# A graph attention layer on one core: where output parts are moved, and how the last two batches of edges are summed

## The chip, the cores and the metric

The kernel runs on one core of a Trainium2 chip. The metric is device time in microseconds (us) for one execution: the median of several runs. A core has a matrix engine (PE), a vector engine (DVE), an activation engine (ACT), a general engine (Pool) and a queue engine (SP); each works through its own queue in order and waits for others by semaphores. PE reads SBUF and writes PSUM; DVE and ACT read and write both. A matmul on float32 appears as two records in the trace.

## The reference, cut to what matters

A layer of graph attention: 12,500 nodes of 128 features, 412,500 edges sorted by target, 4 heads of 32.

```python
h = (relu(layernorm(x)) @ W_node.T).reshape(num_nodes, H, HD)
e = (edge_attr_64 @ W_edge.T).reshape(num_edges, H, HD)
att = leaky(sum(concat([h[src], h[tgt], e]) * a))         # one value an edge and head
m = max(segment_max(att, tgt), 0.0)
ex = exp(att - m[tgt])
denom = segment_sum(ex, tgt) + (num_edges - deg) * exp(-m)
out = x + segment_sum((ex / denom[tgt]) * h[src], tgt)
```

## The kernel before, in words

A first stage normalizes the nodes and writes a table to HBM with one row of 144 floats a node: per head the 32 projected features, two ones and the source's share of the attention value (AW = 35 floats a head, 140 in all), then the target's shares.

The edges are cut into 461 chunks of 896, and the chunks into 58 batches of 8 (CB); the last batch, number 57, has 5 chunks, the fifth of 3 tiles instead of 7 (a tile is 128 edges). NBT is 58. For each batch these steps run:

- `load` and `gather` (L469 to L502): SP fetches edge features and targets; Pool issues one indirect DMA a tile (L500), 56 a batch, that brings the sources' table rows into `hs`. There are two `hs` buffers. From the third batch on a small Pool copy, `gate` (L498), stands in front of a batch's gathers; it reads `sums`, which ACT writes when the batch that last used this buffer has been summed.
- `begin` (L509 to L534): masks (`mem`, `hot`) on DVE and attention values `z` on PE (L518, L521).
- `weigh` (L536 to L565): once all rows have landed, DVE transposes the sources' shares (L541), and DVE and ACT compute leaky values, running maxima and exponentials. It ends with two transposes on DVE (L563, L564).
- `scatter` (L567 to L590): DVE multiplies each chunk's rows by their exponentials (L578, one instruction a chunk); PE then sums the edges of a chunk into its 32 target rows, one matmul a tile (L586), with the mask `hot` as weights. Three chunks (G = 3) go together: a matmul with 96 weight columns and 420 moving columns, of whose nine 32x140 blocks only the three on the diagonal are wanted. In the last two batches the step is one chunk: 32 weight columns, 140 moving columns. The PSUM tile `pa` has two buffers which take turns.
- `collect` (L594 to L609): ACT copies the wanted blocks, four of 32x35 a chunk, from PSUM to the tile `r` (L609). In the last batch's last chunk every other copy is DVE's (L607).
- `merge` (L611 to L656): DVE and ACT join the chunks' sums of one or two batches and add them to `acc`. Batches 0 to 55 are merged in pairs, 56 and 57 each by itself.
- `finish` (L696 to L733): when all edges of some blocks of 128 nodes are in, they are divided by the denominator (`wgt`), brought from the layout (head, node in window) by rows to the layout (node) by rows, added to x and stored. The change of layout is 16 matmuls against parts of the identity (L721), four heads times four partition groups, each in a column group of PE of its own by `tile_position`; DVE adds from PSUM (L726). `parts()` cuts the 98 blocks into thirteen parts of 7, one of 5 and one of 2. The parts of 7 are done behind batches 5, 9, 13 and so on to 53, the part of 5 behind batch 56, that of 2 behind 57. The stores are issued one batch later.

The order is the program's own (`manual_schedule`). In iteration b stand: load and gather of batch b + 1, weigh of b, stores, scatter of b, begin of b + 1, merge of b, finish. So every engine's queue has batch b's scatter, merge and part in front of batch b + 1's weigh. The code behind the loop (`window`) handles chunks whose targets spread too far; with this data it runs no time.

## Time and profile before

| what | us |
|---|---|
| median of 3 runs | 4163.02 (4162.63 to 4165.32) |
| the profiled execution's own time | 4160.05 |
| its span, first to last instruction | 4157.8 |
| Pool busy | 3073.5, of it L500 3047.1 in 3223 gathers |
| DVE busy | 1814.1 |
| PE busy | 1538.9, of it L586 906.3 |
| ACT busy | 645.9, of it L609 385.3 in 1842 copies |

The span begins and ends with the first and last instruction; a little of the time lies around it. The mean granted PE clock over the span is 0.678 of full speed. Rows of the timeline give the start in us, the duration, engine, line, operation, output and input, the number of instructions merged into the row, and in brackets the idle time in front and what ended it.

### The profile page before, as it was taken

What the parts mean: (1) busy time and instruction counts of PE and PEld (TensorE: products, weight loads), DVE (VectorE), ACT (ScalarE), POOL (GpSimd) and SP (SyncE); (2) the same over time, 40 slices, a digit from 0 to 9 for tenths busy, and PEclk for the clock granted to TensorE, in tenths of its full rate; (3) what the DMA queues carried; (4) which work ended last, traced back from release to release, by engine and by line L of the source; (5) the groups of instructions that cost most, each with busy time, mean ns of one, the idle gap of its engine ahead of it and who ended that gap; (6) DMA issues with size and microseconds to landing.
All of it is one profiled execution on the core that took longest, in us unless ns stands there. A gap on an engine that the chain in (4) does not pass through costs nothing.

```text
span 4157.8 us, 24120 instructions
## 1 busy us (share of the span) xinstructions
PE 1538.9 (37%) x4721; PEld 637.2 (15%) x4721; DVE 1814.1 (44%) x3336; ACT 645.9 (16%) x2553; POOL 3073.5 (74%) x3337
## 2 busy tenths in 40 slices
PE   5324252424242524243434333333333242424243
PEld 4101120111110201111111111111111111111112
DVE  8244444434442534353435343534353434434445
ACT  5111111111111111111111111111111111111111
POOL 3777777777777777777777777777777777777774
PEclk8667676767676766666666666676767676767676
DMA  6433433333333333334333333333333333333331
GB/s 183 135 92 96 127 113 94 113 98 107 101 109 99 103 110 94 118 89 118 94 114 98 114 93 118 89 119 94 114 98 114 93 118 90 117 96 109 101 108 51
DMA packets 243629, 440.90 MB, mean 106 GB/s; under 512 B 93947, under 2 KB 144119, under 8 KB 243479
## 3 DMA queue, kind: packets, MB, share of 16 engines
q0 software_dynamic: 103136, 237.83, 21.8%
q1 hardware_dynamic: 127030, 194.11, 14.0%
q10 hardware_dynamic: 13312, 7.36, 0.6%
q8 instruction: 45, 0.74, 0.1%
q14 instruction: 106, 0.86, 0.1%
HBM read 423.75 MB, written 15.29 MB: 106 GB/s over the span
## 4 chain that ended last, share of the span: by engine, by line
POOL 71%; issue 25%; DVE 2%; DMA 1%; PE 1%; ACT 0%; POOLq 0%; DVEq 0%; ACTq 0%
POOL hs L500 71%; DMA hs<-table,src 1%; PE pa L586 1%; DVE stats L265 0%; POOL gate L498 0%; DVE hT L311 0%; DMA table<-rows 0%; DVE hn L297 0%; PE ph L316 0%; PE pt L306 0%; DMA pens<-pen 0%; DVE dif L274 0%; DVE acc L656 0%; DMA xg<-in_x 0%; PE up L721 0%
## 5 line engine op out<-in xcount | busy, mean ns | idle before, releaser
L500 POOL DMA_INDIRECT hs<-table,src x3223 | 3047.1, 945 | 978.2 <-issue 969.3
L586 PE MATMUL pa<-hs,hot 128*96 128x420 f32 (+2 forms) x2526 | 906.3, 523 | 2434.8 <-issue 2345.9
L586 PEld LDWEIGHTS pa<-hs,hot 128*96 128x96 f32 (+2 forms) x2526 | 421.2, 171 | 2931.9 <-issue 2792.2
L541 DVE STREAM_TRANSPOSE zst<-hs 128x224 f32<-128x224 f32 x58 | 33.6, 579 | 1651.6 <-DMA hs<-table,src 1651.6
L609 ACT COPY r<-pa 32x35 f32<-32x35 f32 x1842 | 385.3, 209 | 820.4 <-PE pa L586 800.6
L578 DVE TENSOR_TENSOR hs<-hs,exr 128x924 f32<-128x924 f32 x461 | 476.8, 1101 | 0.0
L550 ACT ACTIVATE a<-z 32x224 f32<-32x224 f32 x232 | 80.5, 347 | 2046.2 <-DVE z L549 2046.2
L518 PE MATMUL z<-eft,wa 128*32 128x384 f32 (+1 forms) x928 | 361.5, 543 | 21.7 <-DMA twb<-table 21.7
L533 DVE TENSOR_TENSOR hot<-exr,key 128x448 f32<-128x448 f32 x231 | 138.7, 622 | 351.8 <-PE pa L586 347.3
L521 PE MATMUL z<-mem,twb 128*32 128x512 f32 x464 | 185.2, 542 | 3.3 <-DMA twb<-table 3.3
L559 ACT ACTIVATE both<-a 32x224 f32<-32x224 f32 x232 | 89.9, 388 | 370.1 <-DVE a L556 365.8
L518 PEld LDWEIGHTS z<-eft,wa 128*32 128x32 f32 x928 | 97.7, 110 | 269.3 <-issue 269.3
L513 DVE TENSOR_TENSOR mem<-mem,exr 128x896 f32<-128x896 int32 x116 | 120.3, 1074 | 18.9 <-DMA mem<-in_dstc 18.9
L549 DVE TENSOR_TENSOR z<-z,zst 32x224 f32<-32x224 f32 x232 | 89.7, 387 | 81.6 <-ACT a L550 76.2
L656 DVE TENSOR_TENSOR acc<-acc,a 128x70 f32 x461 | 109.0, 236 | 33.1 <-DVE acc L656 18.2
L553 DVE TENSOR_TENSOR_SCAN up<-pen,z 32x896 f32<-32x896 f32 x58 | 117.0, 2016 | 2.0
L555 DVE TENSOR_TENSOR_SCAN m<-pen,up 32x896 f32<-32x896 f32 x58 | 116.4, 2007 | 2.0
L561 DVE SCALAR_TENSOR_TENSOR both<-pen,m 32x224 f32<-32x224 f32 x232 | 88.0, 379 | 2.4
L721 PE MATMUL up<-a,ident 128*32 128x224 f32 (+2 forms) x480 | 43.8, 540 | 96.1 <-DVE a L714 96.1
L551 DVE TENSOR_TENSOR z<-z,a 32x896 f32<-32x896 f32 x58 | 63.0, 1087 | 24.0 <-ACT a L550 24.0
L521 PEld LDWEIGHTS z<-mem,twb 128*32 128x32 f32 x464 | 51.2, 110 | 128.0 <-issue 117.4
L556 DVE TENSOR_TENSOR a<-z,m 32x896 f32<-32x896 f32 x58 | 62.5, 1078 | 2.0
(140 smaller groups left out, 732.1 us busy)
## 6 DMA issues: line engine op xcount, KB each, us to landing
eft<-in_ef SPq DMA_DIRECT2D x58, 1792.0 KB
mem<-in_dstc SPq DMA_DIRECT2D x116, 448.0 KB
hs<-table,src POOLq DMA_INDIRECT x3223, 2.5
twb<-table SPq DMA_DIRECT2D x464, 0.5 KB
pen<-pens SPq DMA_DIRECT2D x58, 112.1 KB
xg<-in_x SPq DMA_DIRECT2D x14, 448.0 KB
table<-rows ACTq DMA_DIRECT2D x9, 648.0 KB
out<-xg SPq DMA_DIRECT2D x13, 448.0 KB
```

The lines of the kernel that those rows point to most:

```text
L500: nc.gpsimd.indirect_dma_start(out=s.hs[:, i, :], out_offset=None, in_=table[:, :], in_offset=bass.IndirectOffsetOnAxis(ap=s.src[:, i:i + ...
L513: nc.vector.tensor_tensor(s.mem[:, k, :], s.mem[:, k, :].bitcast(I32), nid_ps[:, pair:pair + 1].to_broadcast([P, CE]), op=OP.is_equal)
L518: nc.tensor.matmul(s.z[:, part], wa3[:, j, :], s.eft[:, j, part], start=(j == 0), stop=False)
L521: nc.tensor.matmul(s.z[:, part], twb[:, s.b % 2, k, :], s.mem[:, k, part], start=False, stop=(k == 1))
L533: nc.vector.tensor_tensor(hot[:, :, q0:q0 + 2, :].rearrange("p t q r -> p q t r"), rows_ps[:, None, None, :].to_broadcast([P, 2, T, W]), k ...
L553: nc.vector.tensor_tensor_scan(up, s.pen[:, :CE], s.z, 0.0, op0=OP.add, op1=OP.max)
L555: nc.vector.tensor_tensor_scan(m[:, ::-1], s.pen[:, CE:0:-1], up[:, ::-1], 0.0, op0=OP.add, op1=OP.max)
L559: nc.scalar.activation(both[g * R:(g + 1) * R, 0, :, :], grouped(att, g), AF.Exp)
L578: nc.vector.tensor_tensor(rows, rows, ex_ps[:, :n, q * H:(q + 1) * H, None].to_broadcast([P, n, H, HB]), op=OP.mult)
L586: nc.tensor.matmul(pa[:v * W, :v * H * AW], hot[:, i, q0:q0 + v, :].rearrange("p q r -> p (q r)"), by_chunk[:, q0:q0 + v, i, :], start=(i ...
L609: nc.scalar.copy(to, pa[q * W:(q + 1) * W, k:k + AW])
L656: nc.vector.tensor_tensor(cols, cols, put[:, i0 + i, :, :], op=OP.add)
```

## The change

Three edits. `finish` gets a flag `by_act`, set for parts behind batches below 56: the 16 matmuls become 16 ACT copies from `w4` to the same places in PSUM. Batch 56 goes in steps of G = 3 as the batches in front of it do. Batch 57 goes in steps of two chunks; chunk q is summed in column group q % 4 of PE into PSUM rows of its own, slot q // 4, the matmuls of the two chunks alternating, and all five chunks use one PSUM tile. `collect` is handed the blocks to copy in place of the tile.

```diff
@@ scatter
-        step = G if s.b + 2 < NBT else 1
+        single = s.b + 1 == NBT
+        step = 2 if single else G
+        if single:
+            one = ps.tile([P, G * H * AW], F32, name="pa", bufs=2)
+            by_slot = one[:, :2 * H * AW].rearrange("p (j k) -> p j k", j=2)
...
+            if single:
+
+                for i in range(T):
+                    for q in range(q0, q0 + w):
+                        if i < held[q]:
+                            g = q % 4
+                            nc.tensor.matmul(by_slot[g * W:(g + 1) * W, q // 4, :], hot[:, i, q, :], by_chunk[:, q, i, :],
+                                             start=(i == 0), stop=(i == held[q] - 1), tile_position=(0, g * W))
+                collect(s, q0, w, [by_slot[q % 4 * W:(q % 4 + 1) * W, q // 4, :] for q in range(q0, q0 + w)])
+                continue
...
-            order = [0, *range(n, T if w > 1 else n), *range(1, n)]
+            order = [0, *range(n, T), *range(1, n)]
...
-            collect(s, q0, w, pa)
+            collect(s, q0, w, [pa[q * W:(q + 1) * W, q * H * AW:(q + 1) * H * AW] for q in range(w)])
@@ collect
-    def collect(s, q0, w, pa):
+    def collect(s, q0, w, blocks):
...
-                k = (q * H + h) * AW
+                what = blocks[q][:, h * AW:(h + 1) * AW]
                 if s.b == NBT - 1 and q0 + w == s.chunks and h % 2:
-                    nc.vector.tensor_copy(to, pa[q * W:(q + 1) * W, k:k + AW])
+                    nc.vector.tensor_copy(to, what)
                 else:
-                    nc.scalar.copy(to, pa[q * W:(q + 1) * W, k:k + AW])
+                    nc.scalar.copy(to, what)
@@ finish
-    def finish(pool, psum, tag, em, b0, n):
+    def finish(pool, psum, tag, em, b0, n, by_act=False):
...
         for h in range(H):
             for s in range(4):
+                if by_act:
+                    nc.scalar.copy(po[s * W:(s + 1) * W, h // 2, h % 2, :n, :], w4[h * W:(h + 1) * W, :n, s, :])
+                    continue
                 nc.tensor.matmul(po[s * W:(s + 1) * W, h // 2, h % 2, :n, :],
...
@@ the loop over batches
-                    stores.append(finish(work, ps, "up", em_ps, b0, n))
+                    stores.append(finish(work, ps, "up", em_ps, b0, n, b + 2 < NBT))
```

More of the change, by code (lines that the diff above doesn't have):

```diff
@@ L579, in scatter @@
                     rows, rows, ex_ps[:, :n, q * H:(q + 1) * H, None].to_broadcast([P, n, H, HB]), op=OP.mult)
+            if single:
[7 more added lines that the diff above has]
+                continue
             pa = ps.tile([P, G * H * AW], F32, name="pa", bufs=2)
             n = held[q0 + w - 1]
-            order = [0, *range(n, T if w > 1 else n), *range(1, n)]
+            order = [0, *range(n, T), *range(1, n)]
             for i in order:
                 v = w if i < n else w - 1
-                nc.tensor.matmul(pa[:v * W, :v * H * AW], hot[:, i, q0:q0 + v, :].rearrange("p q r -> p (q r)"), by_chunk[:, q0:q0 + v, i, :],
-                                 start=(i == order[0]), stop=(i == order[-1]))
-            collect(s, q0, w, pa)
+                nc.tensor.matmul(pa[:v * W, :v * H * AW], hot[:, i, q0:q0 + v, :].rearrange("p q r -> p (q r)"),
+                                 by_chunk[:, q0:q0 + v, i, :], start=(i == order[0]), stop=(i == order[-1]))
+            collect(s, q0, w, [pa[q * W:(q + 1) * W, q * H * AW:(q + 1) * H * AW] for q in range(w)])
     merged = {}
-    def collect(s, q0, w, pa):
+    def collect(s, q0, w, blocks):
         first, last = merge_of(s.b)
         if s.b + 2 < NBT and q0 + w == s.chunks:
-            nc.scalar.copy(sums, pa[:W, 0:1])
+            nc.scalar.copy(sums, blocks[-1][:, 0:1])
         if s.b == first and q0 == 0:
```

## The prediction

> **What bounds the kernel now.** I read the shares by engine first, then the chain of waits, then the group of the gathers, then the last 140 us in order of time. The first three say that Pool's gathers set the pace:

> ```profile
> PE 1538.9 (37%) x4721; PEld 637.2 (15%) x4721; DVE 1814.1 (44%) x3336; ACT 645.9 (16%) x2553; POOL 3073.5 (74%) x3337
> ...
> POOL 71%; issue 25%; DVE 2%; DMA 1%; PE 1%; ACT 0%; POOLq 0%; DVEq 0%; ACTq 0%
> ...
> L500 POOL DMA_INDIRECT hs<-table,src x3223: 940/944/1923, 80.2 to 4111.1; - x190
> ...
> L541 DVE STREAM_TRANSPOSE zst<-hs 128x224 f32<-128x224 f32 x58 | 33.6, 579 | 1651.6 <-DMA hs<-table,src 1651.6
> ```

> From 80 us to 4112 us Pool issues 3223 gathers of 0.945 us with 0.30 us of its own issue time between them, 1.25 us apiece (3223 x 1.25 = 4029). The shortest takes 0.940, the median 0.944, and busy time less count times median is 3047.1 - 3042.5 = 4.6 us: contention costs Pool next to nothing, so relieving it can give next to nothing. DVE waits for the gathers at the head of nearly every batch, 1651.6 / 57 = 29 us a time. The one wait that could stop Pool is the gate copy (L498), which reads `sums`, written at the end of the scatter before. In order of time:

> ```profile
> 4036.58 0.15 ACT L596 COPY sums<-pa 32x1 f32<-32x1 f32 x1 [0.85 <-PE pa L586]
> ...
> 4073.10 0.20 POOL L498 COPY gate<-sums 32x1 f32<-32x1 f32 x1
> ```

> `sums` is there 36.5 us before the gate reads it. So up to the last gather every other engine has room, and only what follows batch 56's arrival can be read as time. There the chain leaves Pool:

> ```profile
> 4074.74 0.58 DVE L541 STREAM_TRANSPOSE zst<-hs 128x224 f32<-128x224 f32 x1 [21.00 <-DMA hs<-table,src]
> ...
> 4087.18 0.58 DVE L564 STREAM_TRANSPOSE hs<-both 128x224 f32<-128x224 f32 x1
> ...
> 4088.97 15.58 PE L586 MATMUL pa<-hs,hot 128*32 128x140 f32 x112 [43.35 <-DVE hs L578]
> ...
> 4105.49 0.17 DVE L621 TENSOR_SCALAR mc<-r 128x8 f32<-128x8 f32 x1 [3.46 <-ACT r L609]
> ...
> 4111.14 0.99 POOL L500 DMA_INDIRECT hs<-table,src  x1 [0.30 <-issue]
> ...
> 4116.33 0.57 DVE L541 STREAM_TRANSPOSE zst<-hs 128x224 f32<-128x224 f32 x1
> ...
> 4130.34 9.42 PE L586 MATMUL pa<-hs,hot 128*32 128x140 f32 x62 [14.88 <-issue]
> ...
> 4140.70 0.21 DVE L607 COPY r<-pa 32x35 f32<-32x35 f32 x1 [0.28 <-ACT r L609]
> ```

> Batch 57's last gather starts at 4111.14 and lands 2.47 us later (as the one at 4072.15 did, by the chain), at 4113.6; its weighing starts at 4116.33 with no idle time in front, because DVE is still busy with batch 56's merge and output part. So batch 56 already ends last, by 2.7 us, and what is added to it from 4088 on is paid in full, as is what is added to batch 57. What stands behind 4140.9 (merge, output part, store) keeps its instructions.

> **The change part by part. (1) Output by ACT copies.** `by_act` holds for the parts behind batches below 56: the thirteen of seven blocks. The parts behind 56 and 57 keep their matmuls. Each of the thirteen loses 16 matmuls and gains 16 copies of 32x224, each waiting for the one before by a semaphore. No row has this copy. Nearest below is a PSUM-to-SBUF ACT operation of that shape (L550, 0.347), nearest above the Exp of that shape with the same wait on ACT (L559: four in 1.62, 0.405 apiece); a SBUF-to-PSUM operation of 528 elements (L629) took 0.61 and is a far upper bound. I take 0.405: 16 x 0.405 = 6.5 us (5.6 to 9.8) against 3.3 us of PE. DVE's L726 waits 3.2 us longer (2.3 to 6.5). In ACT's queue stands next only the following batch's L550, in DVE's the following L541. What hides it: after the part at 3912 DVE idles 17.96 us before L541. If that cover were gone, the 36.5 us of the gate come next; a copy would have to take (3.3 + 18 + 36.5) / 16 = 3.6 us to stop Pool. The last such part is behind batch 53, so none reaches the tail. The SP queue is unmoved: the store is issued an iteration later, behind the pen load. Cost 0.

> **(2) Batch 56 in threes.** Removed: 56 matmuls of 140 columns and eight collects of 4 copies; added: 21 matmuls (14 of 420, 7 of 280 columns) and collects of 12, 12 and 8. Batch 55 already ran so:

> ```profile
> 4017.22 0.58 DVE L564 STREAM_TRANSPOSE hs<-both 128x224 f32<-128x224 f32 x1
> ...
> 4021.01 15.48 PE L586 MATMUL pa<-hs,hot 128*96 128x420 f32 x42 [44.74 <-issue]
> ...
> 4038.42 0.17 DVE L621 TENSOR_SCALAR mc<-r 128x16 f32<-128x16 f32 x1 [1.12 <-ACT r L609]
> ```

> PE's time is the same (15.48 against 15.58), since three times the columns take three times as long. But PE begins after three multiplies instead of one, and 8 copies instead of 4 follow its last matmul. From L564's start to L621: 21.20 in threes, 18.31 in ones; less 0.1 for the `sums` copy that batch 56 lacks, **+2.8 us**, all of it on the path. The bounds come from the same two rows, +2.5 to +3.0. The z matmuls of batch 57 end 2.0 us later, at 4115.6, still ahead of their reader, now at 4119.7.

> **(3) Batch 57 by column groups, in pairs.** Same 31 matmuls (62 records), but pairs of chunks alternate between two column groups, all in one PSUM tile. Two costs and one gain. Cost: the pair's alternation stops at its second matmul until the second multiply, 1.0 us later (4131.3 on the old clock). Cost: in the instruction order of the changed program the first matmul of pair 2, and that of the fifth chunk, wait for a count on ACT which only the last copy of the pair before brings; the tile is tracked as a whole. Before, two tiles took turns and PE never stopped. Queued behind the waiting matmul is all of the scatter. Gain: groups may overlap. The windows show what decides the sizes (us, PE, PEld, DVE, ACT, POOL, then the granted clock):

> ```profile
> 4114.17:4115.46 1.29, 1.29 (x32) 0.97 (x32) 0.00 (x0) 0.00 (x0) 0.00 (x0) 1.00 0.04 13
> 4115.50:4130.30 14.80, 0.00 (x0) 0.00 (x0) 12.57 (x19) 2.94 (x8) 0.00 (x0) 0.55 0.10 28
> 4130.34:4133.80 3.46, 3.46 (x15) 2.63 (x16) 3.45 (x4) 0.00 (x0) 0.00 (x0) 0.50 0.00 0
> 4133.80:4135.70 1.90, 1.90 (x16) 1.71 (x15) 0.00 (x0) 0.83 (x4) 0.00 (x0) 0.90 0.00 0
> 4135.70:4139.80 4.10, 4.06 (x35) 3.48 (x32) 0.00 (x0) 2.36 (x12) 0.00 (x0) 1.00 0.00 0
> ```

> A record of 140 columns takes 3.45 / 14 = 0.246 at clock 0.50 and 1.67 / 14 = 0.119 at 1.00. The output part's 32 records of 160 columns over four groups took 0.040 each where 160 / 140 x 0.119 = 0.136 would be one alone: 3.4-fold overlap on four groups. For two groups I take 1.9 (bounds 1 and 2). Overlap bought at the price of copies in series then gives, on the old clock: pair 1 from 4131.3, 26 records x 0.246 / 1.9 = 3.4, to 4134.7; 8 copies 1.8 (batch 55's eight took 1.76), to 4136.5; pair 2 at full clock 28 x 0.119 / 1.9 = 1.75, with 0.1 for the wait to 4138.4 (at half clock 3.6, to 4140.2); copies, 1.8; chunk five, 6 records, 0.7 or 1.5; its four copies, alternating between ACT and DVE, 0.95. End 4141.9 with the clock up, 4144.5 with it down, against 4140.9: +1.0 to +3.6. A stretch's mean clock dates the step in it: 0.90 over 1.90 us puts the rise at 4134.2, 3.8 us after PE started; 0.55 over 14.8 us puts the fall 1.5 us after PE stopped; 0.80 over the 7.8 us behind 4139.8 puts the next fall 4.7 us after. So a gap of 1.8 us may or may not drop it. I take pair 2 at full clock and chunk five at half, **+1.8 us**.

> [...]

> **Sum:** 0 + 2.8 + 1.8 = +4.6 us, on the profiled execution's 4157.8 span and 4160.05 time (2.97 below the median shown, 4163.02). On the median: 4167.6, or 0.11% up. Own bounds: +2.5 + 0.7 (two-fold overlap) to +3.0 + 3.6, that is 4166.2 to 4169.6.

> **Rivals.** (A) Nothing lost in batch 57: the copies of a pair hide after all, or pair 1 gets the full clock early. Then overlap wins 1.5 us (PE ends at 4137.3, last copies at 4139.4) and the sum is +1.3: 4164.3. For it: overlap is in the trace. Against it: the wait on ACT is in the program. (B) Slower: the two groups do not overlap and every gap drops the clock. Place: the last batch; 26, 28 and 6 records at 0.246 make 14.8 us of PE, with 3.8 of copies between and 0.95 behind from 4131.3: end 4150.8, +9.9, with batch 56 +12.7: 4175.7. It decides "slower" from +5.5 us in this stage on. Against it: the 3.4-fold overlap, and that continuous work raised the clock within 4.2 us each time. Without overlap but with the clock up from pair 2 on it is some 7 us in sum, 4170. (C) ACT's copies stop the gathers: 3.6 us a copy needed, 0.4 expected; each further us per copy would then cost 13 x 16 = 208 us. (D) Faster by more than 8 us: the whole contention of the gathers is 4.6 us, so nothing in the profile pays for it.

> **How the numbers follow.** Forecast 0.76; A 0.09; B 0.10 with its milder form; C 0.01; D 0.04. What a measurement here can tell from no change is about 0.2%, 8.3 us, so forecast, A and the milder half of B are "same": 0.87, with 0.09 slower and 0.04 faster. The time is the forecast's, 4167.6; the range runs from below A, by the runs' own spread of 1 us, to between B's two forms: 4163.3 to 4172.

> **What would show it.** Gathers unchanged at 0.945 and 1.25 apart; the thirteen copies groups near 6.5 us with DVE still idle some 15 us before L541; batch 56 with L564 to L621 near 21; batch 57's L541 near 4119; PE there in three bursts, with gaps of about 1.9 us that end with ACT. I am wrong if the span moves by more than 8 us, if Pool waits at a gate, or if PE's last scatter has no gaps.

## The result, and the profile after

The changed kernel took 4169.92 us in the median of 20 runs (4167.26 to 4171.43), the kernel before 4163.53 (4161.63 to 4165.32): a ratio of 1.0015, 95% interval 1.0009 to 1.0021, so 4 to 9 us longer. The forecast was 4167.6, or 4.6 us more than the 4163.02 it started from; the medians of 20 runs differ by 6.4 us.

The profiled execution took 4170.56 us, its span is 4168.8. First the page of the changed kernel: shares of the chain of waits, then groups (busy us and mean ns of one, then the idle time in front and what ended it).

```profile
POOL 72%; issue 24%; DVE 2%; PE 1%; DMA 1%; ACT 0%; SPq 0%; POOLq 0%; DVEq 0%; ACTq 0%
...
L500 POOL DMA_INDIRECT hs<-table,src x3223 | 3050.7, 947 | 978.2 <-issue 972.6
...
L541 DVE STREAM_TRANSPOSE zst<-hs 128x224 f32<-128x224 f32 x58 | 33.6, 578 | 1616.8 <-DMA hs<-table,src 1616.8
...
L736 ACT COPY up<-a 32x224 f32<-32x224 f32 x208 | 70.7, 340 | 33.4 <-DVE a L728 27.2
```

Pool still sets the pace, and DVE still waits 1616.8 / 57 = 28 us for each batch's gathers. The part behind batch 53 in order of time, first in the kernel before:

```profile
3915.38 1.16 DVE L726 TENSOR_TENSOR xg<-up,xg 128x448 f32<-128x448 f32 x2 [3.42 <-PE up L721]
...
3934.50 0.58 DVE L541 STREAM_TRANSPOSE zst<-hs 128x224 f32<-128x224 f32 x1 [17.96 <-DMA hs<-table,src]
```

then in the changed kernel:

```profile
3918.11 5.92 ACT L736 COPY up<-a 32x224 f32<-32x224 f32 x16 [2.09 <-DVE a L728]
...
3924.06 1.16 DVE L743 TENSOR_TENSOR xg<-up,xg 128x448 f32<-128x448 f32 x2 [6.04 <-ACT up L736]
...
3940.58 0.58 DVE L541 STREAM_TRANSPOSE zst<-hs 128x224 f32<-128x224 f32 x1 [15.36 <-DMA hs<-table,src]
```

Sixteen copies take 5.92 us; DVE's add waits 6.04 us instead of the 3.42 it waited for PE, and the idle time in front of the next transpose falls from 17.96 to 15.36: 2.6 us taken out of slack, nothing out of the end. The last two batches:

```profile
4093.33 0.58 DVE L564 STREAM_TRANSPOSE hs<-both 128x224 f32<-128x224 f32 x1
...
4097.11 16.27 PE L600 MATMUL pa<-hs,hot 128*96 128x420 f32 x42 [45.53 <-issue]
...
4115.22 0.27 DVE L635 TENSOR_SCALAR mc<-r 128x8 f32<-128x8 f32 x1 [3.94 <-ACT r L623]
...
4117.05 1.11 POOL L500 DMA_INDIRECT hs<-table,src  x1 [0.30 <-issue]
...
4126.15 0.57 DVE L541 STREAM_TRANSPOSE zst<-hs 128x224 f32<-128x224 f32 x1
...
4138.53 0.58 DVE L564 STREAM_TRANSPOSE hs<-both 128x224 f32<-128x224 f32 x1
...
4140.16 0.65 PE L590 MATMUL pa<-hs,hot 128*32 128x140 f32 x2 [14.87 <-issue]
4141.13 3.04 PE L590 MATMUL pa<-hs,hot 128*32 128x140 f32 x26 [0.33 <-DVE hs L582]
4144.21 1.75 ACT L623 COPY r<-pa 32x35 f32<-32x35 f32 x8 [6.17 <-PE pa L590]
4146.01 1.86 PE L590 MATMUL pa<-hs,hot 128*32 128x140 f32 x28 [1.84 <-ACT r L623]
4147.95 1.78 ACT L623 COPY r<-pa 32x35 f32<-32x35 f32 x8 [1.99 <-PE pa L590]
4149.78 0.90 PE L590 MATMUL pa<-hs,hot 128*32 128x140 f32 x6 [1.91 <-ACT r L623]
```

Batch 56 takes 21.89 us from L564 to the merge's first reader of the copies, where the ones took 18.31. Batch 57's transpose has no idle time in front, 9.1 us behind its last gather's start (5.2 before): the delay is paid in full. In batch 57 PE runs its first two records, and the third waits for the second multiply; then PE works in three bursts, and both gaps between them, 1.84 and 1.91 us, end with ACT: PE and ACT take turns. From L541 of batch 56 to the end of the span it is 87.9 us, 83.1 before: **+4.85 us** in the stretch that holds the edits to the last two batches. The rest of this pair of profiles, 6.15 us in front of that, is no step of the change: the first gather starts 2.4 us later (82.69 against 80.25) and first to last gather is 3.5 us longer (4034.4 against 4030.9). The experiments say how far these two belong to the change.

### The profile page after: what moved, and what is told of

Read it like the earlier page. It is cut to its first block, busy times and chain, and to the rows that moved or that the text cites. A ratio compares the mean times of both kernels' runs of the same rounds, so it can differ in the third digit from the quotient of the medians.

```text
span 4168.8 us, 23404 instructions
## 1 busy us (share of the span) xinstructions
PE 1496.2 (36%) x4235; PEld 608.4 (15%) x4235; DVE 1813.4 (43%) x3336; ACT 722.2 (17%) x2761; POOL 3077.2 (74%) x3337
## 4 chain that ended last, share of the span: by engine, by line
POOL 72%; issue 24%; DVE 2%; PE 1%; DMA 1%; ACT 0%; SPq 0%; POOLq 0%; DVEq 0%; ACTq 0%
POOL hs L500 71%; PE pa L600 0%; DVE stats L265 0%; DMA hs<-table,src 0%; POOL gate L498 0%; DMA table<-rows 0%; PE ph L316 0%; DVE hT L311 0%; DVE hn L297 0%; PE pa L590 0%; PE pt L306 0%; ACT r L623 0%; DMA twb<-table 0%; DMA pens<-pen 0%; DVE acc L670 0%
## 5 line engine op out<-in xcount | busy, mean ns | idle before, releaser
L500 POOL DMA_INDIRECT hs<-table,src x3223 | 3050.7, 947 | 978.2 <-issue 972.6
L600 PE MATMUL pa<-hs,hot 128*96 128x420 f32 (+1 forms) x2394 | 895.6, 537 | 2553.8 <-issue 2510.1
L600 PEld LDWEIGHTS pa<-hs,hot 128*96 128x96 f32 (+1 forms) x2394 | 406.7, 175 | 3054.4 <-issue 2918.9
L541 DVE STREAM_TRANSPOSE zst<-hs 128x224 f32<-128x224 f32 x58 | 33.6, 578 | 1616.8 <-DMA hs<-table,src 1616.8
L550 ACT ACTIVATE a<-z 32x224 f32<-32x224 f32 x232 | 80.5, 347 | 1939.5 <-DVE z L549 1939.5
L559 ACT ACTIVATE both<-a 32x224 f32<-32x224 f32 x232 | 89.9, 388 | 370.0 <-DVE a L556 365.8
L561 DVE SCALAR_TENSOR_TENSOR both<-pen,m 32x224 f32<-32x224 f32 x232 | 87.9, 379 | 2.4
L736 ACT COPY up<-a 32x224 f32<-32x224 f32 x208 | 70.7, 340 | 33.4 <-DVE a L728 27.2
L551 DVE TENSOR_TENSOR z<-z,a 32x896 f32<-32x896 f32 x58 | 63.0, 1087 | 23.9 <-ACT a L550 23.9
```

The lines of the kernel that those rows point to most:

```text
L500: nc.gpsimd.indirect_dma_start(out=s.hs[:, i, :], out_offset=None, in_=table[:, :], in_offset=bass.IndirectOffsetOnAxis(ap=s.src[:, i:i + ...
L559: nc.scalar.activation(both[g * R:(g + 1) * R, 0, :, :], grouped(att, g), AF.Exp)
L600: nc.tensor.matmul(pa[:v * W, :v * H * AW], hot[:, i, q0:q0 + v, :].rearrange("p q r -> p (q r)"), by_chunk[:, q0:q0 + v, i, :], start=(i ...
```

## The experiments

Each kernel was timed beside the kernel before on the same chip. The three groups ran on three different chips: beside `e1` to `e4` and `e9` to `e12` the kernel before took 5116 and 5112 us, beside `e5` to `e8` it took 4160. Where it took over 5100 the matrix engine is at times far slower, also while batch 56 is weighed (23.9 us from its L541 to its L564 in `e12_before_again`, 12.4 in the first profile), but not from that L564 on, 70 to 76 us before the end. So the scatters of the last two batches can be read from all of the profiles, total times only against the kernel before of the same group.

**One part at a time.** `e1_act_only` is the kernel before with the edit to `finish` alone:

```diff
-    def finish(pool, psum, tag, em, b0, n):
+    def finish(pool, psum, tag, em, b0, n, by_act=False):
...
             for s in range(4):
+                if by_act:
+                    nc.scalar.copy(po[s * W:(s + 1) * W, h // 2, h % 2, :n, :], w4[h * W:(h + 1) * W, :n, s, :])
+                    continue
                 nc.tensor.matmul(po[s * W:(s + 1) * W, h // 2, h % 2, :n, :],
...
-                    stores.append(finish(work, ps, "up", em_ps, b0, n))
+                    stores.append(finish(work, ps, "up", em_ps, b0, n, b + 2 < NBT))
```

> Only the output parts by ACT copies, both scatters as before. Theory (the thirteen parts are hidden): no change, 4163.5 within 1 us of the kernel before; the copies take 5.9 us a part, DVE still idles 15 us before the next transpose, gathers busy 3047 us in sum, and the stretch from batch 56's first transpose (L541) to the last store is 75.0 us as before. Rival (ACT's copies slow the gathers, which in the changed kernel's profile were busy 3.6 us longer in sum): +3 us or more, gathers busy near 3051.

4806.27 us against 5116.12, ratio 0.9396 (0.9369 to 0.9423): 310 us shorter, which neither theory had. Whether the parts are hidden as forecast can't be told here, because the cover that the forecast names is not there: Pool waits at its gate (below). The gathers are busy 3055.9 us in sum, but 3055.2 in `e2_threes_only`, which has no ACT copies: the sum does not tell the rival from chance.

`e2_threes_only`:

```diff
-        step = G if s.b + 2 < NBT else 1
+        step = G if s.b + 1 < NBT else 1
```

> Only batch 56 in threes, output parts and batch 57 as before. Theory (three multiplies first, eight copies last, all on the path): +2.8 to +3.6 us, from the transpose L564 to the first instruction of the merge that reads the copies 21.2 to 21.9 us instead of 18.3, and batch 57's L541 later by the same. Rival (the delay is taken up behind batch 56, because batch 57 waits for something else): 0 to +1.

5111.32 against 5116.12, ratio 1.0006 (0.9983 to 1.0030): the time shows nothing at this spread. The profile does:

```profile
5026.89 0.58 DVE L564 STREAM_TRANSPOSE hs<-both 128x224 f32<-128x224 f32 x1
...
5047.90 0.17 DVE L621 TENSOR_SCALAR mc<-r 128x8 f32<-128x8 f32 x1 [3.94 <-ACT r L609]
...
5058.73 0.57 DVE L541 STREAM_TRANSPOSE zst<-hs 128x224 f32<-128x224 f32 x1
```

From L564 to the merge's first reader it is 21.01 us, a little under the 21.2 to 21.9 of the theory, and batch 57's L541 follows with no idle time in front, 31.84 us behind L564 instead of 29.15: the delay is not taken up behind batch 56.

`e3_pairs_only` is the changed kernel with batch 56 in ones and the output parts by matmuls:

```diff
-        step = 2 if single else G
+        step = 2 if single else G if s.b + 2 < NBT else 1
...
-                    stores.append(finish(work, ps, "up", em_ps, b0, n, b + 2 < NBT))
+                    stores.append(finish(work, ps, "up", em_ps, b0, n))
```

> Only batch 57 by column groups in pairs in one PSUM tile. Theory (pairs overlap 1.9-fold, and PE stops twice for ACT's copies): +0.9 us, up to +3.6 if the clock is down for pair 2; PE in three bursts with gaps near 1.85 us that ACT ends. Rival (the groups don't overlap): +4.6. Rival (the stops cost nothing): -1.5.

```profile
5103.75 3.47 PE L590 MATMUL pa<-hs,hot 128*32 128x140 f32 x26 [0.33 <-DVE hs L582]
...
5109.08 1.86 PE L590 MATMUL pa<-hs,hot 128*32 128x140 f32 x28 [1.85 <-ACT r L623]
...
5112.85 0.90 PE L590 MATMUL pa<-hs,hot 128*32 128x140 f32 x6 [1.91 <-ACT r L623]
```

In the profile the stage from batch 57's L564 to the merge's first instruction took 13.58 us, three bursts of PE with ACT between; the kernel before takes 12.21. Total 5133.06 against 5116.12, ratio 1.0035 (1.0017 to 1.0052), 17 us; the stage accounts for under 2 of them, and what the rest is stays open.

`e4_pairs_two_tiles` is `e3_pairs_only` with the tile taken anew for each pair:

```diff
-        if single:
-            one = ps.tile([P, G * H * AW], F32, name="pa", bufs=2)
-            by_slot = one[:, :2 * H * AW].rearrange("p (j k) -> p j k", j=2)
...
             if single:
-
+                one = ps.tile([P, G * H * AW], F32, name="pa", bufs=2)
+                by_slot = one[:, :2 * H * AW].rearrange("p (j k) -> p j k", j=2)
                 for i in range(T):
```

> Batch 57 by column groups in pairs, but each pair in a PSUM tile of its own, two taking turns; the rest as before. Theory (the stops came from the one tile): PE runs pair 2 at once behind pair 1, the copies follow each other on ACT, and the scatter of batch 57 is 9.8 us from its first multiply to the last copy instead of 11.8 before and 12.7 with one tile: -2.0 us against the kernel before, 2.9 us under the pairs in one tile. Rival (ACT's 20 copies bound the stage whatever PE does): as the pairs in one tile.

Its last scatter in order of time:

```profile
5107.20 4.68 PE L588 MATMUL pa<-hs,hot 128*32 128x140 f32 x54 [0.33 <-DVE hs L579]
5110.71 3.81 ACT L621 COPY r<-pa 32x35 f32<-32x35 f32 x17 [6.61 <-PE pa L588]
5112.53 0.90 PE L588 MATMUL pa<-hs,hot 128*32 128x140 f32 x6 [0.65 <-ACT r L621]
```

The 54 records of both pairs follow each other without a gap and the copies run in one piece on ACT; only the fifth chunk, which takes the first tile again, still waits 0.65 us for ACT. The stage takes 10.66 us, 2.9 less than with one tile, as the theory had it, and 1.5 less than the kernel before, where the theory had 2.0. The tile is all that differs between the two kernels: the gaps came from the one tile, and the rival falls. The total doesn't follow the stage: 5126.84 against 5116.12 (1.0026, 1.0009 to 1.0043) is 10.7 us longer than the kernel before, though 6 under the pairs in one tile, and that too stays open.

**The whole, the parts, and a better version, with the kernel before at 4160.03.** `e5_act_only_again` is the kernel of the first experiment.

> The same edit as in the first experiment, output parts by ACT copies alone, in the hope of PE working as it did in the first profiles. If the kernel before takes about 4163: theory (hidden): no change within 1 us; rival (ACT's copies slow the gathers): +2 to +3.6 with the gathers' busy sum near 3051. If the kernel before takes about 5116 as in the first four: 4806 again, 13 parts x 24 us less.

4161.11, ratio 1.0002 (0.9993 to 1.0011). The last batches take 83.2 us, as before, and first to last gather takes 4030.8 us where the kernel before took 4030.9, with the same 3047.1 us of busy gathers: ACT's copies don't slow the gathers here. The thirteen parts are hidden, within what this can resolve (-3 to +5 us).

`e6_changed_again` is the changed kernel as it is.

> The changed kernel itself. With PE as in the first profiles: +4.7 us from the last two batches (3.6 in front of batch 57, 0.9 in its scatter, 0.2 behind), and from the gathers between 0 (they scatter from run to run) and +3.6 (they are slower by the change). With PE as in the first four: as the ACT copies alone plus 5, near 4811.

4167.16, ratio 1.0016 (1.0007 to 1.0025), +7.1 us. Its profile is that of its longest run, 4176.88 us; gathers from first to last take 4039.8 us there, but batches 56 and 57 show something of their own. The windows (us, PE, PEld, DVE, ACT, POOL, granted clock):

```profile
4145.30:4148.80 3.50, 3.46 (x26) 2.38 (x26) 2.47 (x3) 0.00 (x0) 0.00 (x0) 0.50 0.00 0
4148.80:4150.60 1.80, 0.00 (x0) 0.00 (x0) 0.00 (x0) 1.67 (x8) 0.00 (x0) 0.50 0.00 0
4150.60:4154.20 3.60, 3.47 (x28) 2.41 (x28) 0.00 (x0) 0.05 (x1) 0.00 (x0) 0.54 0.00 0
```

The clock did not rise in pair 1, so pair 2 took 3.47 us instead of 1.86, and the stage 15.17 instead of 13.13. Against the 12.21 of the kernel before that is +3.0 with pair 2 at half clock; the four other profiles with pairs in one tile have it at full clock and lie 0.9 to 1.4 above. So both cases that the prediction named occur, the one at full clock in four of five profiles.

`e7_pairs_in_both` is the kernel before with both last batches in pairs, each pair in its own tile (`single = s.b + 2 >= NBT`, and the tile as in `e4_pairs_two_tiles`):

> Kernel before with batches 56 and 57 by column groups in pairs, each pair in a PSUM tile of its own. Theory: batch 56 from L564 to the merge's first reader 13 us instead of 18.4, of which 2.7 us are a gain, since batch 57's weighing then waits for its gathers; batch 57's scatter 10.0 instead of 11.8; in sum -4 to -5 us where PE works as in the first profiles, 4159. Rival (DVE's chain, not the gathers' landing, still ends last in front of batch 57): -7.

4156.91, ratio 0.9991 (0.9982 to 1.0000), -3.1 us, short of the -4 to -5 expected. In order of time:

```profile
4091.24 4.43 PE L588 MATMUL pa<-hs,hot 128*32 128x140 f32 x54 [0.18 <-DVE hs L579]
...
4101.96 0.17 DVE L633 TENSOR_SCALAR mc<-r 128x8 f32<-128x8 f32 x1
4115.95 0.58 DVE L541 STREAM_TRANSPOSE zst<-hs 128x224 f32<-128x224 f32 x1 [3.07 <-DMA hs<-table,src]
```

Batch 56 takes 13.33 us instead of 18.3, and batch 57's transpose now waits 3.07 us for its gathers: of 5 us won, the last 3 end in that wait, and the rival (-7) falls. The theory had 2.7 us of them as a gain. It is 1.9, because the transpose starts 3.30 us behind the last gather's start (5.19 in the kernel before), where 2.47 had been taken for the landing. Batch 57's stage takes 10.67 us. From L541 of batch 56 to the end it is 79.7 us, 3.4 less than before and 8.2 less than in the changed kernel.

`e8_pairs_in_both_act` adds the ACT copies to that.

> As the one before, and the thirteen output parts by ACT copies. Theory: the same time as without the copies where PE works as in the first profiles, and some 300 us less, near 4801, where it works as in the first four experiments.

4157.86, ratio 0.9993 (0.9984 to 1.0002); last batches 79.7 us. The two kernels' times lie within each other's spread.

**Again with the slower matrix engine.** `e9_threes_only_again` and `e10_pairs_only_again` are the second and third kernels again, `e12_before_again` is the kernel before, and `e11_act_on_the_path` is, against its name, the changed kernel once more.

> Batch 56 in threes alone, as in the second experiment, with the kernel before near 4160. Theory: +2.6 to +3.6 us, 4163 (ones have taken 17.7 to 18.8 us from L564 to the merge's first reader, threes 21.0 to 21.9). No further fall of PE's clock in the first stage (it fell there at 67 to 68.5 us in all five profiles with ACT's output copies and in none of five without): first gather at 80 to 81 us. Rival (that fall is chance): it may come here too.

> Batch 57 in pairs in one tile alone, as in the third experiment, with the kernel before near 4160. Theory: +0.9 us where the clock is up for pair 2, +3 where it is down, the median between, 4161 to 4163. First gather at 80 to 81 us; the rival as for the threes.

> [...]

> The kernel before itself, to see what no change looks like: ratio 1 within 0.0005, no fall of the clock at 67 to 69 us in the first stage, first gather at 80 to 81 us, gathers busy 3040 to 3044 us in sum. Rival (the fall is chance): it falls here too.

Ratios 1.0005 (0.9989 to 1.0020), 1.0034 (1.0020 to 1.0047) and, for the kernel before against itself, 1.0007 (0.9994 to 1.0019), which is 5 us with no change at all; the pairs in one tile are 17 us longer for the second time, on another chip, and this stays unexplained. The changed kernel took 4817.97 in its one run against 5111.66. Stages: threes 22.09 us in batch 56; pairs in one tile 13.53 and, in the changed kernel, 13.14 us in batch 57. The suspicion that ACT's copies go with a later fall of the clock in the first stage, and so with a later first gather, falls: the clock also fell at 67 us in the other three of these runs, which have no such copies, and not in `e11_act_on_the_path`, which has. First gathers start at 79.7 to 81.6 us without the copies and at 81.0 to 82.8 with them; whether a shift of a microsecond is left is open. What goes with a later first gather is the fall itself: 81.3 to 82.8 us in the eight profiles that have it, 79.7 to 81.3 in the six that don't.

**Why the same change is 294 us shorter where PE is slow.** Pool's waits, first `e12_before_again` (us in total, times, longest):

```profile
POOL gate L498 <- ACT sums L596: 890.2, 56, 40.1
```

then `e11_act_on_the_path`:

```profile
POOL gate L498 <- ACT sums L610: 587.0, 56, 16.8
```

The gate, which was never late in the first profile, now stops Pool in every batch from the third on, and 303 us of that go with the change. One output part in `e12_before_again`, in order of time:

```profile
2047.95 3.22 PE L721 MATMUL up<-a,ident 128*32 128x224 f32 x32 [13.94 <-issue]
...
2107.50 1.15 DVE L726 TENSOR_TENSOR xg<-up,xg 128x448 f32<-128x448 f32 x2 [59.70 <-remote]
2108.57 0.57 DVE L541 STREAM_TRANSPOSE zst<-hs 128x224 f32<-128x224 f32 x1
...
2140.48 0.18 POOL L498 COPY gate<-sums 32x1 f32<-32x1 f32 x1 [37.60 <-ACT sums L596]
```

All 32 records of the part's matmuls run within 3.2 us, yet DVE's add waits 59.7 us and starts 56 us behind their end ("remote" is a releaser that the view can't name). The add also needs `xg`, but that load was issued at 1971.15, long before; in the trace the semaphore that the last of these matmuls raises goes up at 2107.47, so it is PE's result that comes late. The z matmuls before the part are stretched as well, two records of 512 columns here:

```profile
2024.23 1.01 PE L521 MATMUL z<-mem,twb 128*32 128x512 f32 x1 [1.79 <-issue]
...
2027.73 1.01 PE L521 MATMUL z<-mem,twb 128*32 128x512 f32 x1 [2.49 <-issue]
```

They start 3.5 us apart; in the first profile eight such records take 3.17 us together, at a granted clock of 1.00. After the late add, weighing is late, so `sums` is late, and the gate holds Pool for 37.6 us. In `e11_act_on_the_path` a part looks as it did with PE at its usual pace:

```profile
1955.60 5.92 ACT L736 COPY up<-a 32x224 f32<-32x224 f32 x16 [2.09 <-issue]
1961.55 1.16 DVE L743 TENSOR_TENSOR xg<-up,xg 128x448 f32<-128x448 f32 x2 [6.04 <-ACT up L736]
```

If all of the 303 us come from the parts, 303 / 13 = 23 us a part reach Pool, of the 54 us by which this add comes earlier. This is the prediction's own chain (late part, late weighing, late `sums`, gate), reached from PE's side. Why PE is slow in these runs was not found; both groups that show it ran on other chips than the one that doesn't.

## Why the prediction was right, point by point

**Output parts, cost 0: right.** The copy was sized at 0.405 us with its wait and is 0.37 (5.92 / 16); 2.6 us of slack are used where 3.2 were expected, and the parts alone give 1.0002 (0.9993 to 1.0011). The cover named, idle DVE in front of L541 and the gate's 36.5 us, is what this rests on: in the runs where it is gone, a part's delay reaches the time of the kernel, 23 us of 54.

**Batch 56 in threes, +2.8 us: right in place, mechanism and size.** By the rows above, PE starts 3.78 us behind L564 instead of 1.79 (three multiplies first), and the merge's reader comes 1.84 us behind PE's last record instead of 0.94 (eight copies): +2.9 us. The other 0.7 of the 3.6 us measured is PE itself, 16.27 us against 15.58, because the granted clock rose 5.5 us after its start instead of 4.2. This start at half clock explains the spread of all profiles: ones took 17.65 us with 2.9 us of it and 18.80 with 5.25, threes 21.01 with 3.75 and 22.09 with 5.9, so each us of it adds 0.49, and at the same length of it threes cost 2.95 more than ones. The plain means are 18.4 (seven profiles) and 21.6 (five), +3.2. That batch 56 ends last also held, though by less than the 2.7 us stated: by `e7_pairs_in_both` its lead over the gathers is 1.9.

**Batch 57, +1.8 us: the mechanism is right, the size is a compromise that none of the profiles shows.** The terms hold: overlap of two groups 1.8-fold (28 records in 1.86 us, 0.066 each, against 0.119), where 1.9 was taken; gaps 1.84 and 1.91 where 1.9 was taken. The clock is what differs. The forecast took pair 2 at full clock and the fifth chunk at half; the fifth chunk ran at full clock in every profile, and pair 2 did in all but one. In the profile of the result the step cost 0.9 us (13.13 against 12.21), just under the forecast's own +1.0; with pair 2 at half clock it cost 3.0. The means, 12.0 us in ones (six profiles, 11.63 to 12.21) and 13.7 in pairs in one tile (five, 13.13 to 15.17), differ by 1.7, but only because one of the five is the long case: that this is near 1.8 is luck. The wait on ACT for the whole tile, read from the changed program, is what `e4_pairs_two_tiles` removes, and with it the sign turns: 10.66, 1.4 under the mean of the ones. Rival A's sum would have come near with that tile; rival B's missing overlap is refuted.

**The sum.** In the pair of profiles 3.6 + 0.9 and 0.3 of small shifts elsewhere make the 4.85 us, close to the forecast's 4.6 because batch 56 came out 0.8 over it and batch 57 0.9 under; that they cancel is luck too. The medians differ by 6.4 us, with 4 to 9 by the ratio's interval. What is left, some 1.5 us, is in no step of the prediction, and no run places it. The gathers' 3.5 us in the pair of profiles do not come with the copies (4030.8 us in `e5_act_only_again`, as before; 4032.0 in `e8_pairs_in_both_act` against 4031.4 without copies in `e7_pairs_in_both`). The later first gather is open. Both pairs that differ by the copies alone came out 1 us longer with them, which is within the spread of the runs. What the prediction had not seen is how much its "nothing" of the first part depends on PE's pace: where PE is slow, that part alone decides the sign, by 300 us.

## What to carry to other kernels

Work that is off the chain has two prices, one while the cover holds and one when it is gone; name the cover and its size, and look at which engine the step leans on, since the same edit has another price when that engine is slower (here the parts alone: 1 us, within the spread, beside 4160, and 310 us shorter beside 5116). Where two engines should take turns on a result, give each turn a buffer of its own: disjoint rows of one tile still made PE wait for ACT's copies (1.84 and 1.91 us here, and 13.58 us for the stage where a tile for each pair took 10.66). A gain in front of a wait for data is worth only the distance to that data (here 3 of 5 us were lost in it).
